# Norm rows moved into shared pages, sign-weight loads asked for one piece ahead, and the first score steps of an image ordered step by step

## The chip, the core and the metric

The kernel runs on one core of a Trainium2 chip. The metric is device time in microseconds (us) for one execution of the whole program. The profile comes from one further execution, recorded by the hardware profiler. A core has a matrix engine (TensorE, PE in the profile, with its weight loads as PEld), a vector engine (VectorE, DVE), an activation engine (ScalarE, ACT), a general engine (GpSimd, POOL) and a queue engine (SyncE, SP) that only issues transfers. Each runs its own instructions in order and waits on semaphores for the others. TensorE's results land in PSUM, which this kernel uses as eight tiles ("banks") of 128 x 512 floats.

## The reference: what is computed

Eight images of 32 x 32 pixels (1024 tokens) with 384 channels go through two layers. All is float32.

```python
# layer 0: x = x + attention0(group_norm(x))
qkv = gn(x) @ qkv_w + qkv_b                      # 6 heads of 64
attn = einsum('bqd,bkd->bqk', q * 64**-0.5, k)   # 1024 x 1024 per head
attn = attn + rel_h[:, :, :, :, None] + rel_w[:, :, :, None, :]   # position part, from q
x = x + softmax(attn) @ v @ proj_w + proj_b
# layer 1, on tokens t (8, 1024, 384):
t = t + causal_attention(ln(t), Wq, Wk, Wv)      # one head of 384
t = t + ffn(ln(t), W1, b1, W2, b2)               # first 5 images only get a non-zero ffn
# ffn: both weights are replaced by the sign of (w - mean of its group of rows),
#      5 groups by output feature; after each product an absmax scale over a whole image
Wb[g] = sign(W[g] - W[g].mean())
```

(In the feed-forward part the quantization works on groups of one image for images 0 to 4; images 5 to 7 get zeros there.)

## The kernel before

A scheduler places the instructions of each engine in an order that it works out from priorities (the order in which the program asks) and from readiness, and it hands out pool buffers as they come free. An instruction that asks for a buffer waits until the buffer's last user is done. The pools that matter here:

```python
class Pools:
    def __init__(self, ctx, tc, path):
        ...
        self.image_ = pool("image", 11)                        # [128, 3080] floats each
        self.page_ = pool("page", 12 if self.fast else 8)      # [128, 1024] floats each
        self.xn = pool("xn", 3)                                # [128, 384] floats each
        ...
        self.ps_o = pool("ps_o", 8, space=PSUM)                # the eight banks
```

The signs of the feed-forward weights are made once, during image 0, by a generator that the attention code advances with `next` between its own steps. Every weight is read twice: once for the group sums (`"w"`), once for the signs (`"sign"`). The results go to DRAM (`w1s`, `w2s`) and are read back for each image.

```python
PIECES = (                                   # 1.5 MB; 0.75 + 0.75 MB; 1.5 MB
    ((0, w1T, w1s, 0, CUT1, FF),),
    ((0, w1T, w1s, CUT1, NC, FF), (1, w2T, w2s, CUT2, NM, C)),
    ((1, w2T, w2s, 0, CUT2, C),),
)
def binarize(pools):
    def pieces(name):
        for n, piece in enumerate(PIECES):
            room, at = pools.flat(f"{name}_{n}"), 0            # one image buffer
            for i, (which, src, sign, k0, k1, n_out) in enumerate(piece):
                w = room[:, at : ...]
                nc.gpsimd.dma_start(out=w, in_=src...)         # L227
                yield which, w, sign[...], n_out, i + 1 == len(piece)
    ...
    for which, w, _, n_out, _ in pieces("w"):
        yield False
        for g in range(NG):
            nc.vector.tensor_reduce(part[...], w[:, :, ts(g, n_out // NG)], AX.XY, ALU.add)   # L235
        ...
    nc.gpsimd.partition_all_reduce(mean, part, ...)            # L243
    for which, w, dst, n_out, last in pieces("sign"):
        ...   # per group: above = w > mean (L257); w = (w < mean) reversed-subtract above (L258)
        nc.sync.dma_start(out=dst, in_=w)                      # L265
```

The layer norms of layer 1 work on half an image, four rows of tiles each. The normalized row `xn` is transposed on TensorE (three 128 x 128 blocks) and copied out.

```python
for i, j in enumerate(js):                                     # four per half
    xn = pools.xn.tile([P, C], F32, tag="xn", name=f"xn_{name}_{j}")
    nc.vector.tensor_scalar(xn, xt[:, j, :], mv[:, i, 0:1], rs[:, i : i + 1], ALU.subtract, ALU.mult)   # L361
    transpose_tiles(xT[:, half, :, ts(i, P)], [xn[:, ts(k, P)] for k in range(NC)], ...)               # L299
```

Layer 0's attention takes head pairs p = 0, 1, 2 in turn. A **step** is one chunk of 128 keys (c) against 512 queries (half) for the two heads of the pair: its scores fill two banks. Each bank gets a product of queries and keys (L569) and a position part (L573) on top; ScalarE's exponential (L579) then frees the bank. Sixteen steps per pair come in bursts of 2, 3, 3, 3, 3, 2; behind the scores of one burst stand the value products (L590) of the burst before.

```python
def scores(p, c, half):
    sc = [pools.o_tile(...) for par in range(2)]
    for par in range(2):
        nc.tensor.matmul(sc[par], k[rows[par], p, ts(c, P)], q[rows[par], p, ts(half, 512)], start=True, stop=False)   # L569
    for par in range(2):
        nc.tensor.matmul(sc[par], unit[...], r[2 * (c // 4) + c % 2][rows[par], p, ts(half, 512)], start=False, stop=True)   # L573
    pr = pools.page(f"pr0_{b}_{p}_{c}_{half}")
    for par in range(2):
        last_exp[0] = nc.scalar.activation(pr[:, ts(par, 512)], sc[par], AF.Exp).ins      # L579
    return pr
...
if b == 0:
    signs.append(binarize(pools))
for p in range(NPAIR):
    sums = [pools.page(...) for half in range(2)]
    for n, burst in enumerate(bursts):
        prs = [scores(p, *u) for u in burst]
        if b == 0 and (p, n) == (0, 1):
            multiply_out(pools)        # wqk = Wq Wk^T: 9 products in 3 banks (L287), copied out by VectorE (L288)
        for u in pending:
            values(*u)                 # running sum on VectorE (L587), product with v on TensorE (L590)
        if n == 0 and p > 0: few = set_aside(p - 1, *last)
        if b == 0 and xt is None and next(signs[0]) or b > 0 and (p, n) == (1, 1):
            xt = residual()            # loads x; GpSimd adds a bias (L552)
        if p == 0:
            with tc.issue_after(last_exp[0]): next(later, None)    # position parts of pairs 1 and 2: cast (L498), rest (L499), DMAs (L506)
        if n == 2 and p > 0: divide(p - 1, few)                   # a small product into one bank (L622), read by VectorE (L412)
        pending = ...
```

Of the kernel before, what the change touches and what calls it, by code (L numbers as in the profile page):

```python
# [1 line left out]

# [7 lines left out]
F32 = mybir.dt.float32  # L10
# [7 lines left out]
P = 128  # L18
B, H, W, C = 8, 32, 32, 384
# [21 lines left out]
class Pools:  # L41
    def __init__(self, ctx, tc, path):
        self.path, self.fast = path, path == "f"

        def pool(name, bufs, **kw):
            return ctx.enter_context(tc.tile_pool(name=f"{path}_{name}", bufs=bufs, **kw))

        self.image_ = pool("image", 11)
        self.page_ = pool("page", 12 if self.fast else 8)
        self.xn = pool("xn", 3)  # L50
        self.work = pool("work", 2)
        self.small = pool("small", 3)
        self.ps_o = pool("ps_o", 8, space=PSUM)
# [20 lines left out]
def conv_attn_hybrid(  # L74
# [19 lines left out]
    nc = tc.nc  # L94
# [72 lines left out]
    unit = const.tile([P, 2, HB, WB], F32R, name="unit")  # L167
# [49 lines left out]
# [6 lines that stand above are left out]
                room, at = pools.flat(f"{name}_{n}"), 0  # L223
                for i, (which, src, sign, k0, k1, n_out) in enumerate(piece):
                    w = room[:, at : at + (k1 - k0) * n_out].rearrange("p (k o) -> p k o", o=n_out)
                    at += (k1 - k0) * n_out
                    nc.gpsimd.dma_start(out=w, in_=src.rearrange("(k p) o -> p k o", p=P)[:, k0:k1, :])  # L227
                    yield which, w, sign[:, k0 * n_out : k1 * n_out], n_out, i + 1 == len(piece)

        part = const.tile([P, 2, 2, NG], F32, name="sums_w")  # L230
        times = [0, 0]
        for which, w, _, n_out, _ in pieces("w"):
            yield False
            for g in range(NG):
                nc.vector.tensor_reduce(  # L235
                    part[:, times[which], which, g : g + 1], w[:, :, ts(g, n_out // NG)], AX.XY, ALU.add
                )
            times[which] += 1
            if which == 1 or w.shape[1] > 1:
                yield False  # L240
        nc.vector.tensor_tensor(part[:, 0], part[:, 0], part[:, 1], ALU.add)
        mean = const.tile([P, 2, NG], F32, name="mean_w")
        nc.gpsimd.partition_all_reduce(  # L243
            mean.rearrange("p a g -> p (a g)"), part[:, 0].rearrange("p a g -> p (a g)"), P, bass_isa.ReduceOp.add
        )
        for which, n in enumerate((FF // NG * C, C // NG * FF)):
            nc.vector.tensor_scalar_mul(mean[:, which], mean[:, which], 1.0 / n)
        done = 0
        for which, w, dst, n_out, last in pieces("sign"):
            gs = n_out // NG  # L250
            step = min(C // gs, w.shape[1])
            for k in range(0, w.shape[1], step):
                for g in range(NG):
                    wg, m = w[:, k : min(k + step, w.shape[1]), ts(g, gs)], mean[:, which, g : g + 1]
                    above = pools.xn.tile([P, C], F32, tag="xn", name=f"above_{which}_{n_out}")
                    above = above[:, : wg.shape[1] * gs].rearrange("p (k o) -> p k o", o=gs)
                    nc.vector.tensor_scalar(above, wg, m, None, ALU.is_gt)  # L257
                    nc.vector.scalar_tensor_tensor(wg, wg, m, above, ALU.is_lt, ALU.subtract, reverse1=True)  # L258
                    done += wg.shape[1] * gs
                    if done > 600:  # L260
                        done = 0
                        yield False
            if NG * gs < n_out:
                nc.vector.memset(w[:, :, NG * gs :], 0.0)
            nc.sync.dma_start(out=dst.bitcast(F32), in_=w.rearrange("p k o -> p (k o)"))  # L265
            if last:
                yield True
# [22 lines left out]
    def stages(pools):  # L290
# [3 lines left out]
        def transpose_tiles(dst, srcs, engine):  # L294

            n = len(srcs)
            pt = pools.o_tile("pt")
            for i, s in enumerate(srcs):
                last_transpose[0] = nc.tensor.transpose(pt[:, ts(i, P)], s, ident).ins  # L299
            engine(dst, pt[:, : n * P].rearrange("p (i q) -> p i q", i=n))  # L300
# [37 lines left out]
        def layer_norm_T(xt, xT, half, name, xlo=None):  # L338

            js = range(4 * half, 4 * half + 4)  # L340
            mv = pools.small.tile([P, 4, 2], F32, tag="lmv", name=f"lmv_{name}_{half}")
            for i, j in enumerate(js):
                st = pools.small.tile([P, 6], F32, tag="lst", name=f"lst_{name}_{j}")
                nc.vector.bn_stats(st, xt[:, j, :])
                nc.vector.bn_aggr(mv[:, i, :], st)
            sd = pools.small.tile([P, 4], F32, tag="lsd", name=f"lsd_{name}_{half}")
            nc.vector.tensor_scalar_add(sd, mv[:, :, 1], 1e-5)
            nc.scalar.activation(sd, sd, AF.Sqrt)
            rs = pools.small.tile([P, 4], F32, tag="lrs", name=f"lrs_{name}_{half}")
            nc.vector.reciprocal(rs, sd)  # L350

            def hi_lo(i):
                def place(dst, ps):
                    nc.scalar.copy(dst, ps)
                    nc.vector.tensor_tensor(xlo[:, half, :, ts(i, P)], ps, dst.bitcast(F32), ALU.subtract)

                return place

            for i, j in enumerate(js):
                xn = pools.xn.tile([P, C], F32, tag="xn", name=f"xn_{name}_{j}")  # L360
                nc.vector.tensor_scalar(xn, xt[:, j, :], mv[:, i, 0:1], rs[:, i : i + 1], ALU.subtract, ALU.mult)  # L361
                transpose_tiles(
                    xT[:, half, :, ts(i, P)], [xn[:, ts(k, P)] for k in range(NC)], nc.scalar.copy if xlo is None else hi_lo(i)
                )
            return rs
# [62 lines left out]
        def layer0(b, xT):  # L428


            q, k = (pools.image(f"{n}_{b}") for n in ("q", "k"))


            r = [pools.image(f"r_{b}_{part}", F32R) for part in range(4)]

            rows = (slice(0, HD), slice(HD, P))
# [87 lines left out]
            for m in range(2 * NPAIR):  # L524
                queries_keys(m)
                if 0 < m <= NPAIR:
                    near.append(positions(m - 1))
                if m == NPAIR and unfinished:
                    unfinished.pop()()

                    early = pools.small.tile([P, 1], F32, tag="early", name=f"early0_{b}")
                    nc.scalar.activation(early, k[:, 0, T - 1 :], AF.Exp, scale=0.0)
            for j in range(NJ):
                values(j)
            for _ in place(0, *near[0]):
# [21 lines left out]
        def attend0_fast(residual, b, q, k, r, v, later):  # L557
# [2 lines left out]
            oT = pools.image(f"oT_{b}")  # L560

            rows = (slice(0, HD), slice(HD, P))
            last_exp = [None]

            def scores(p, c, half):

                sc = [pools.o_tile(f"s0_{b}_{p}_{c}_{half}_{par}") for par in range(2)]
                for par in range(2):
                    nc.tensor.matmul(  # L569
                        sc[par], k[rows[par], p, ts(c, P)], q[rows[par], p, ts(half, 512)], start=True, stop=False  # L570
                    )
                for par in range(2):
                    nc.tensor.matmul(  # L573
                        sc[par], unit[rows[par], c // 2 % 2].rearrange("i h w -> i (h w)"),
                        r[2 * (c // 4) + c % 2][rows[par], p, ts(half, 512)], start=False, stop=True,
                    )
                pr = pools.page(f"pr0_{b}_{p}_{c}_{half}")
                for par in range(2):
                    last_exp[0] = nc.scalar.activation(pr[:, ts(par, 512)], sc[par], AF.Exp).ins  # L579
                return pr  # L580
# [59 lines left out]
                    nc.vector.tensor_tensor(oT[:, p, ts(half, 512)], avs[half], rb[:, ts(half, 512)], ALU.mult)  # L640

            xt = None
            if b == 0:
                signs.append(binarize(pools))

            units = [(c, half) for c in range(NJ) for half in range(2)]
            bursts = [units[at : at + n] for at, n in zip(BURSTS_AT, BURSTS)]
# [1 line left out]
            for p in range(NPAIR):  # L649
# [19 lines left out]
                last = (sums, avs)  # L669
# [71 lines left out]
        def attention1(xt, more, b, between, start):  # L741
# [14 lines left out]
            for j in range(7):  # L756
                more(j)
            layer_norm_T(xt, xT, 0, f"1_{b}")
            for j in range(7, NJ):
                more(j)  # L760
# [209 lines left out]
        signs = []  # L970
        unfinished = []

        def run(pools):
# [5 lines left out]
            if pools.fast:  # L979
                make_unit(pools)  # L980
            for b in range(B):
                xt, more = layer0(b, gn)

                def between():
# [32 lines left out]
    with ExitStack() as scope:  # L1017
        pools = Pools(scope, tc, "f")
# [43 lines left out]
```

## Time and profile before

| what | value |
|---|---|
| median of three executions | 2452.15 us (2447.83 to 2455.35) |
| span of the profiled execution | 2457.7 us |
| ScalarE busy | 1032.6 us (42%) |
| VectorE busy | 1393.6 us (57%) |
| GpSimd busy | 275.2 us (11%) |
| mean granted TensorE clock | 0.990 |
| period of one image: a projection of layer 0 (L423) in image 1 to the same one in image 2 (388.63 to 715.93 us) | 327.30 us |
| image 0: score steps of layer 0 to its output projection (72.13 to 205.06 us) | 132.9 us |
| image 1: the same stretch (429.07 to 532.95 us) | 103.9 us |

Read it so: busy time is what an engine's own records cover; a busy TensorE may still be running its products in a poor order, because the ends of pipelined products are modelled. The waits list tells, for each engine, what ended its idle times. The timeline gives start, length and, in square brackets, the idle time just before. A number after x is a count of instructions; one float32 product is two of them, one of the float32r products one. L numbers are lines of the kernel.

### The profile page before, as it was taken

The page shows a single profiled execution, that of the slowest core. Times are in us where ns is not written, and L with a number is a line of the kernel's source. Part 1 is how long each engine was busy: PE and PEld are TensorE (multiplying, and loading weights), DVE is VectorE, ACT ScalarE, POOL GpSimd, SP SyncE. Part 2 cuts the span into 40 slices and gives each one's busy share as a digit, 9 for nine tenths or more (in the row PEclk, how much of TensorE's full clock was granted, in tenths as well). Part 3 has the DMA queues.
Part 4 walks back from the last instruction along what each step waited for, and adds up shares of the span by engine and source line. Part 5 has one row for each costly group of instructions (what it writes and reads, how often), then busy time and mean ns, then how long its engine had stood idle before and what let it go on. Part 6 is the DMA issues. An engine that isn't in the chain of part 4 may idle for free.

```text
span 2457.7 us, 25707 instructions
## 1 busy us (share of the span) xinstructions
PE 2400.5 (98%) x9378; PEld 1286.1 (52%) x9378; DVE 1393.6 (57%) x2182; ACT 1032.6 (42%) x1756; POOL 275.2 (11%) x389
## 2 busy tenths in 40 slices
PE   7899999999999999999999999999999999999998
PEld 3334576345674356843457634567435543554344
DVE  4577555773475754557635577346575257524751
ACT  3342264632465513745226463246551155125520
POOL 0230001300013000022000130001300021001200
PEclk9899999999999999999999999999999999999999
DMA  7622206310127011082110631012700271017100
GB/s 160 197 82 99 103 1 125 107 53 12 39 77 155 27 38 39 1 172 69 55 39 1 128 104 54 12 39 77 155 26 1 64 155 40 0 43 143 47 1 28
DMA packets 154792, 169.97 MB, mean 69 GB/s; under 512 B 113408, under 2 KB 126048, under 8 KB 153120
## 3 DMA queue, kind: packets, MB, share of 16 engines
q1 hardware_dynamic: 134416, 98.93, 17.6%
q0 software_dynamic: 17184, 69.22, 9.4%
q8 instruction: 77, 1.26, 0.2%
q10 hardware_dynamic: 3056, 0.08, 0.1%
q14 instruction: 59, 0.48, 0.1%
HBM read 75.38 MB, written 42.47 MB: 48 GB/s over the span
## 4 chain that ended last, share of the span: by engine, by line
PE 95%; DVE 2%; DMA 1%; ACT 1%; issue 0%; POOL 0%; DVEq 0%; ACTq 0%
PE f_s L569 14%; PE f_av L590 14%; PE f_qk L423 10%; PE f_av L805 8%; PE f_s L792 8%; PE f_y L952 7%; PE f_y L911 7%; PE f_v L371 5%; PE f_v L518 5%; PE f_q L749 5%; PE f_s L573 4%; PE f_pj L371 2%; PE f_rel L468 2%; PE f_pj L679 2%; PE f_pt L299 1%; PE f_pj L684 1%
## 5 line engine op out<-in xcount | busy, mean ns | idle before, releaser
L579 ACT ACTIVATE f_pr<-f_s 128x512 f32<-128x512 f32 x768 | 409.2, 597 | 351.8 <-PE f_s L573 295.6
L569 PE MATMUL f_s<-f_q,f_k 64*128 64x512 f32 x1536 | 417.8, 611 | 21.3 <-DVE wqk L288 10.6
L590 PE MATMUL f_av<-f_pr,f_v 128*64 128x512 f32 x1536 | 363.8, 607 | 0.0
L587 DVE TENSOR_TENSOR f_sum<-f_sum,f_pr 128x1024 f32<-128x1024 f32 x288 | 353.8, 1279 | 17.6 <-ACT f_pr L579 17.4
L573 PE MATMUL f_s<-f_r,unit 64*128 64x512 f32 x768 | 310.6, 773 | 0.0
L423 PE MATMUL f_qk<-f_gnT,wqkv_sb 128*128 128x512 f32 x576 | 258.3, 601 | 1.6 <-DVE f_gnT L334 1.6
L569 PEld LDWEIGHTS f_s<-f_q,f_k 64*128 64x128 f32 x1536 | 147.2, 186 | 193.5 <-issue 110.6
L590 PEld LDWEIGHTS f_av<-f_pr,f_v 128*64 128x64 f32 x1536 | 99.1, 137 | 221.5 <-issue 197.2
L805 PE MATMUL f_av<-f_v,f_pr 128*128 128x385 f32 x576 | 203.8, 503 | 0.0
L792 PE MATMUL f_s<-f_q,f_lnT 128*128 128x512 f32 (+3 forms) x576 | 195.9, 488 | 0.0
L423 PEld LDWEIGHTS f_qk<-f_gnT,wqkv_sb 128*128 128x128 f32 x576 | 108.2, 191 | 143.8 <-issue 133.5
L799 ACT ACTIVATE f_pr<-f_s 128x512 f32<-128x512 f32 (+3 forms) x96 | 47.1, 490 | 262.7 <-DVE f_s L797 216.3
L805 PEld LDWEIGHTS f_av<-f_v,f_pr 128*128 128x128 f32 x576 | 112.2, 197 | 81.7 <-issue 19.7
L506 POOL DMA_DIRECT2D f_r<-f_far x192 | 101.3, 530 | 444.7 <-DVE f_far L499 378.0
L792 PEld LDWEIGHTS f_s<-f_q,f_lnT 128*128 128x128 f32 x576 | 102.0, 190 | 77.7 <-issue 54.0
L915 ACT ACTIVATE f_h<-f_y,b_sb 128x256 f32<-128x256 f32 x240 | 100.6, 470 | 67.7 <-PE f_y L911 67.7
L749 PE MATMUL f_q<-f_lnT,wqk 128*128 128x512 f32 x288 | 127.5, 592 | 0.0
L573 PEld LDWEIGHTS f_s<-f_r,unit 64*128 64x128 f32 x768 | 80.5, 188 | 89.7 <-issue 88.7
L371 PE MATMUL f_v<-wv_sb,f_lnT 128*128 128x384 f32 x384 | 126.5, 486 | 0.0
L922 DVE TENSOR_REDUCE am<-f_h 128x1 f32<-128x1024 f32 (+2 forms) x80 | 71.6, 947 | 96.3 <-ACT f_h L915 96.3
L518 PE MATMUL f_v<-wqkv_sb,f_gnT 128*128 128x384 f32 x384 | 125.1, 486 | 0.0
L806 DVE COPY tot<-f_av 128x1 f32<-128x1 f32 x64 | 10.0, 157 | 166.5 <-PE f_av L805 166.5
(162 smaller groups left out, 3071.8 us busy)
## 6 DMA issues: line engine op xcount, KB each, us to landing
f_far<-f_far SPq DMA_DIRECT2D x48, 512.0 KB, 3.4
f_r<-f_far POOLq DMA_DIRECT2D x192, 128.0 KB, 4.1
f_r<-f_far SPq DMA_DIRECT2D x192, 128.0 KB, 3.3
f_gnT<-in_xT SPq DMA_DIRECT2D x24, 512.0 KB, 4.6
f_x<-in_x SPq DMA_DIRECT2D x32, 384.0 KB, 6.3
out_y<-f_x POOLq DMA_DIRECT2D x28, 384.0 KB, 4.6
f_near<-f_far SPq DMA_DIRECT2D x128, 64.0 KB, 4.4
f_w1a<-w1s POOLq DMA_DIRECT2D x5, 1536.0 KB, 7.0
```

The lines of the kernel that those rows point to most:

```text
L371: nc.tensor.matmul(ps[:, :C], xT[:, k, ts(j, P)], w[:, k, cols], start=(k == 0), stop=(k == NC - 1))
L423: nc.tensor.matmul(made[half], wqkv_sb[:, i, ts(m, P)], xT[:, i, ts(half, 512)], start=(i == 0), stop=(i == NC - 1))
L518: nc.tensor.matmul(ps, keys[:, i, j // 2, j % 2], wqkv_sb[:, i, 2 * C :], start=(i == 0), stop=(i == NC - 1))
L569: nc.tensor.matmul(sc[par], k[rows[par], p, ts(c, P)], q[rows[par], p, ts(half, 512)], start=True, stop=False)
L573: nc.tensor.matmul(sc[par], unit[rows[par], c // 2 % 2].rearrange("i h w -> i (h w)"), r[2 * (c // 4) + c % 2][rows[par], p, ts(half, 512) ...
L579: last_exp[0] = nc.scalar.activation(pr[:, ts(par, 512)], sc[par], AF.Exp).ins
L587: nc.vector.tensor_tensor(sums[half], prev, pr, ALU.add)
L590: nc.tensor.matmul(avs[half][ts(par, HD), :], v[:, c, ts(h, HD)], pr[:, ts(par, 512)], start=(c == 0), stop=(c == NJ - 1),)
L749: nc.tensor.matmul(ps, wqk[:, k, ts(m, P)], xT[:, half, k, :], start=(k == 0), stop=(k == NC - 1))
L792: nc.tensor.matmul(sc[:, lo:], xT[:, c // 4, k, ts(c % 4, P)], q[:, half, k, lo:], start=(k == 0), stop=(k == NC - 1),)
L805: nc.tensor.matmul(av[:, : C + 1], prs[c][:, ts(j - c, P)], v[:, c, :], start=(c == 0), stop=(c == j))
L911: nc.tensor.matmul(ps, w1k[i // 2][:, ts(m, P)], xs[i % 2][:, half, i // 2, :], start=(i == 0), stop=(i == 2 * NC - 1))
```

## The change

Four edits are made together.

- The norm rows `xn` are taken from the page pool (12 buffers) instead of from a pool of their own with 3. That pool keeps 2 buffers for the sign work.
- The loads of weights, for sums and for signs, are asked for one piece ahead of the piece being worked on (`one_ahead`).
- For image 0 the generator is started in front of layer 0's value projection, not at the start of the attention, so that its first loads are asked for there.
- In each image's first pair, steps 1 to 4 are tied behind the last position part of the step before: the scheduler may no longer put the query-key products of later steps ahead of an earlier step's position part.

```diff
-        self.xn = pool("xn", 3)
+        self.xn = pool("xn", 2)
...
+        def one_ahead(loads):
+            got = next(loads)
+            for load in loads:
+                yield got
+                got = load
+            yield got
...
-        for which, w, _, n_out, _ in pieces("w"):
-            yield False
+        loads = one_ahead(pieces("w"))
+        got = next(loads)
+        yield False
+        for which, w, _, n_out, _ in itertools.chain([got], loads):
             for g in range(NG):
...
-        for which, w, dst, n_out, last in pieces("sign"):
+        for which, w, dst, n_out, last in one_ahead(pieces("sign")):
...
             for i, j in enumerate(js):
-                xn = pools.xn.tile([P, C], F32, tag="xn", name=f"xn_{name}_{j}")
+                xn = pools.page(f"xn_{name}_{j}")[:, :C]
...
+            if pools.fast and b == 0:
+                signs.append(binarize(pools))
+                next(signs[0])
             for j in range(NJ):
                 values(j)                       # layer 0's value projection
...
-            last_exp = [None]
+            last_exp, last_score = [None], [None]
             def scores(p, c, half):
                 sc = [...]
-                for par in range(2):
-                    nc.tensor.matmul(sc[par], k..., q..., start=True, stop=False)
-                for par in range(2):
-                    nc.tensor.matmul(sc[par], unit..., r..., start=False, stop=True)
+                with tc.issue_after(last_score[0]) if p == 0 and 0 < 2 * c + half < 5 else contextlib.nullcontext():
+                    for par in range(2):
+                        nc.tensor.matmul(sc[par], k..., q..., start=True, stop=False)
+                    for par in range(2):
+                        last_score[0] = nc.tensor.matmul(sc[par], unit..., r..., start=False, stop=True).ins
...
-            if b == 0:
-                signs.append(binarize(pools))
```

More of the change, by code (lines that the diff above doesn't have):

```diff
@@ L1 @@
+import contextlib
+import itertools
 from contextlib import ExitStack
@@ L562, in attend0_fast @@
             rows = (slice(0, HD), slice(HD, P))
-            last_exp = [None]
+            last_exp, last_score = [None], [None]
             def scores(p, c, half):
                 sc = [pools.o_tile(f"s0_{b}_{p}_{c}_{half}_{par}") for par in range(2)]
-                for par in range(2):
-                    nc.tensor.matmul(
-                        sc[par], k[rows[par], p, ts(c, P)], q[rows[par], p, ts(half, 512)], start=True, stop=False
-                    )
-                for par in range(2):
[L573 to L576, printed above, removed]
+                with tc.issue_after(last_score[0]) if p == 0 and 0 < 2 * c + half < 5 else contextlib.nullcontext():
+                    for par in range(2):
+                        nc.tensor.matmul(
+                            sc[par], k[rows[par], p, ts(c, P)], q[rows[par], p, ts(half, 512)], start=True, stop=False
+                        )
+                    for par in range(2):
+                        last_score[0] = nc.tensor.matmul(
+                            sc[par], unit[rows[par], c // 2 % 2].rearrange("i h w -> i (h w)"),
+                            r[2 * (c // 4) + c % 2][rows[par], p, ts(half, 512)], start=False, stop=True,
+                        ).ins
                 pr = pools.page(f"pr0_{b}_{p}_{c}_{half}")
```

## The prediction

> **What bounds the kernel now.** I read the busy table first, then TensorE's waits, then timelines of the places that the change touches. In the busy table the columns are busy time, share of the span and instructions:
>
> ```profile
> span 2457.7 us, 25707 instructions
> PE 2400.5 (98%) x9378; PEld 1286.1 (52%) x9378; DVE 1393.6 (57%) x2182; ACT 1032.6 (42%) x1756; POOL 275.2 (11%) x389
> ```
>
> TensorE is idle for 2457.7 - 2400.5 = 57.2 us only. So no edit that merely fills idle time can bring more than 57 us (2.3%), and the waits say who holds what part of it (total us, times, longest):
>
> ```profile
> PE f_pt L299 <- DVE xn L361: 12.4, 13, 2.0
> PE f_gmean L321 <- DVE gmv L318: 11.3, 1, 11.3
> PE f_s L569 <- DVE wqk L288: 10.6, 1, 10.6
> PE f_s L569 <- ACT f_pr L579: 6.7, 15, 0.5
> PE f_s L569 <- DVE seen L412: 4.0, 1, 4.0
> ```
>
> Lines 1, 3, 4 and 5 belong to the three things changed: norm rows, weight loads (image 0), first score steps. The timeline of TensorE shows more than idle time. Where image 1's scores begin, the scheduler has put the query-key products of four steps ahead of the first position part (start, length; idle before in brackets):
>
> ```profile
> 429.07 3.70 PE L569 MATMUL f_s<-f_q,f_k 64*128 64x512 f32 x16
> 432.21 1.04 PE L573 MATMUL f_s<-f_r,unit 64*128 64x512 f32 x4
> 433.69 1.18 PE L569 MATMUL f_s<-f_q,f_k 64*128 64x512 f32 x3 [0.44 <-ACT f_pr L579]
> ...
> 435.46 1.94 PE L590 MATMUL f_av<-f_pr,f_v 128*64 128x512 f32 x8
> ...
> 437.33 0.73 PE L573 MATMUL f_s<-f_r,unit 64*128 64x512 f32 x4
> ...
> 438.51 1.18 PE L569 MATMUL f_s<-f_q,f_k 64*128 64x512 f32 x3 [0.45 <-ACT f_pr L579]
> ...
> 445.19 1.13 PE L569 MATMUL f_s<-f_q,f_k 64*128 64x512 f32 x4
> ```
>
> All eight banks are opened, none is finished before 432.2, so the first exponential starts at 433.04 and frees banks one at a time. The normal rhythm begins at 445.19.
>
> [...] after the 10.6 us wait twelve value products take 4.94 us, and 2.79 us later; granted clock 0.69 in 84 to 104 us. [...] here a pair of score products passes in about 0.4 us, and pairs break up where banks come free singly (433.69). [...] here a running sum takes 1.2 us, and 2.0 us while GpSimd's bias adds run (138 to 156 us).
>
> **Step 1, score order, images 1 to 7.** In the changed program as built, TensorE's order is step 0 whole, step 1 whole, and so on: the rhythm of all other pairs. From 429.07 to 445.19, 16.12 us, stand 8 score steps and 5 value steps. Their price in the normal rhythm, from distances between starts: three score steps 448.67 - 445.19 = 3.48; three value steps 451.40 - 448.67 = 2.73; two score steps 459.97 - 457.59 = 2.38; two value steps (image 0, 128.99 to 130.86) 1.87. So 2.38 + 3.48 + 1.87 + 3.48 + 2.73 = 13.94, and **2.18 us** are saved per image: 0.9 are the two waits[...]. Two conditions. ScalarE must keep up: its first exponential comes 1.45 us after the first product of a burst (457.59 to 459.04), a step's two take 1.06, and its casts (1.04 and 1.99) stay where they are; laid out from 429.07, step 4 then finds its banks free at 431.6 and needs them at 433.4, and step 7 finds its own at 437.0 and needs them at 438.9. No stall. And the position parts must have landed: parts r_0 and r_1 of pair 0 are issued last at 425.2 to 426.4 on SP and land in 2.4 to 3 us, by 429.5; they would now be wanted at 429.9 and 431.7. 7 x 2.18 = **15.3 us**.
>
> **Step 2, norm rows.** Per image with a feed-forward part the fourth transpose waits for its norm row, which waited for the first row's buffer, which TensorE frees only by transposing:
>
> ```profile
> 620.31 1.15 PE L299 MATMUL f_pt<-ident,xn 128*128 128x128 f32 x9
> ...
> 622.83 0.47 DVE L361 TENSOR_SCALAR xn<-f_x,lmv,lrs 128x384 f32<-128x384 f32 x1
> ...
> 623.45 0.52 PE L299 MATMUL f_pt<-ident,xn 128*128 128x128 f32 x3 [2.00 <-DVE xn L361]
> ```
>
> With four buffers to be had, VectorE's order puts the fourth row right behind the third, at about 616.7, 3.6 us before TensorE wants the first. 5 x 2.0 = 10.0; the other eight waits (2.4 us together, 0.3 each, in the first norm of layer 1) have the same cause. I take 11.4 of 12.4. Pages are not short there: the attention's are done with.
>
> **Step 3, image 0.** Here I expect little. The stretch from scores to output projection takes 132.9 us against 103.9 in image 1; 8.2 of the 29 are real extra products (L273 2.1, L287 6.1). The 10.6 us wait arises so: VectorE stands in its queue at the sums of the first piece, whose load was issued at 84.44 behind position-part DMAs on GpSimd and lands at 95.58, and the copies of wqk, which free three banks, stand behind the sums. In the changed order pieces 0 and 1 (3 MB) are loaded at the very start and summed by 60 us. But piece 2 stands behind the same DMAs (which wait for VectorE's L499, then at about 78), so it is issued at about 82.5 and lands at about 93.5 if it takes 11.1 us again; and VectorE's first sum of it stands **ahead** of the wqk copies still, the copies being mixed with five sums of 0.78. The last bank comes free at 94.3 + 3 x 0.49 + 4 x 0.78 = 98.9. TensorE is then through steps 6 and 7 at about 99.9, and was at 104.25 before: 4.3 gained, not 10.6.
>
> Then VectorE becomes the nearer limit. From 98.9 its order holds, ahead of pair 0's closing transposes: 14 running sums (16.5), two position remainders (3.2), the signs of pieces 0 and 1 (about 20 pairs, 14), then transposes and reductions (4.7): done at about 139 to 140. TensorE wants their result (L622) at 99.9 + 38.0 (the distance 104.25 to 142.29 before) = 137.9. It waits some 2 us, and the wait for a bank behind it (4.0 before) stays at about the same length, since GpSimd's bias adds now fall at about 137 to 155. Gain left: about 2 to 3. Against it stands the start: 3 MB from GpSimd's queue join at about 6 us the loads that hold up the first product (14.78). The scale of the projection weights ends at 12.84, 1.9 us early[...]. I put this at -1. Net for image 0: **+1**, anywhere from -5 to +8.
>
> **Sum.** 15.3 + 11.4 + 1 = 27.7 us; 2452.15 - 27.7 = **2424.4 us**, 1.1% faster.
>
> **Rivals.** (a) Position parts come late: TensorE, no longer fed with query-key products, stands at step 0 or 2. The old order hid up to 3 us of lateness; the margins above are 2 to 5 us. If it happens, step 1 gives nothing: 2440. (b) VectorE takes over in image 0, with signs ahead of running sums: pages fill, exponentials stop, TensorE waits 10 us more than I say: 2435. (c) The start is slowed by 5 us through shared transfers: 2429. (d) Piece 2 arrives early or its sums are not in the way, and the 10.6 us with its throttled clock vanishes: about 10 us more, 2414. (e) TensorE's 2.0 us waits turn into waits for ScalarE's copy out of the bank; that copy takes 0.48 us a row and is not late today, so I give this little.
>
> **Range and chances.** Steps 1 and 2 are sums of repeated, nearly equal pieces (26.7 us); I trust them to within 4. Image 0 gives the width: 2412 to 2438 for 8 in 10. Faster by over 2% means below 2403.1, a gain of 49 us, more than idle time and the reorder together can plausibly give: 0.03. Slower by over 2% would need a stall of 75 us against the gains: 0.01. Within 2%: 0.96.
>
> **What would show it.** In the profile after: no wait of L299 on xn beyond 1 us in total; no L569 wait on f_pr in images 1 to 7, and a distance from an image's first score product to its third burst's first of 14 us, not 16.12; a period from image 1 to image 2 of 327.3 - 2.2 - 2.0 - 0.3 = 322.8 us; the wait on wqk still there, at 6 to 11 us; a wait at L622 or behind it of 4 to 7 us; the first L423 product at 15 to 17 us. Wrong would be: an L573 wait on a DMA of f_r, a wqk wait of under 3 us, VectorE busy without a gap and TensorE waiting for it for more than 8 us in image 0, or a first product after 18 us.

## The result and the profile after

The changed kernel took **2424.7 us** (median of four executions, 2424.4 to 2427.3), the kernel before 2453.75 us beside it (2447.8 to 2459.3): ratio 0.9884, 95% interval 0.9859 to 0.9909. 1.2% faster, within the prediction's range and 0.3 us from its middle. The sum was right, two of its terms were too small, and the third had the wrong sign.

The busy table of the changed kernel (busy time, share of the span, instructions):

```profile
span 2422.6 us, 25725 instructions
PE 2378.5 (98%) x9378; PEld 1274.1 (53%) x9378; DVE 1392.1 (57%) x2182; ACT 1035.4 (43%) x1756; POOL 264.9 (11%) x389
```

The span is 35.1 us shorter (the profiled execution of the kernel before was one of its longer ones). Only 13.1 us of that is idle time of TensorE (57.2 to 44.1); 22.0 us is "busy" time that went although the 9378 products are the same. So most of the gain is in how fast the products pass, and that the table of busy times can't say. TensorE's waits after (total us, times, longest):

```profile
PE f_gmean L333 <- DVE gmv L330: 11.3, 1, 11.3
PE f_qk L435 <- DVE f_gnT L346: 8.4, 1, 8.4
PE f_s L585 <- DVE wqk L300: 8.3, 1, 8.3
PE f_pt L311 <- DVE f_xn L373: 2.4, 8, 0.3
PE f_s L585 <- DVE seen L424: 2.1, 1, 2.1
```

Gone are the five 2.0 us waits for norm rows and every wait of scores for exponentials. The second line has grown from 1.6 us: the first projection product of image 0 starts at 21.57 us, and not at 14.78. Third and fifth line are image 0's waits, 10.6 and 4.0 us before.

TensorE's timeline in image 1 shows the score order: a step's query-key products (L585), then its position part (L589), without a wait:

```profile
426.40 1.13 PE L585 MATMUL f_s<-f_q,f_k 64*128 64x512 f32 x4
426.96 0.80 PE L589 MATMUL f_s<-f_r,unit 64*128 64x512 f32 x2
427.60 1.02 PE L585 MATMUL f_s<-f_q,f_k 64*128 64x512 f32 x4
...
440.12 1.13 PE L585 MATMUL f_s<-f_q,f_k 64*128 64x512 f32 x4
```

From the first product to the third burst it is 440.12 - 426.40 = 13.72 us (16.12 before).

The norm rows of the feed-forward part of image 1, in the same view; first line the kernel before, behind its wait, then the kernel after:

```profile
623.80 11.58 PE L805 MATMUL f_av<-f_v,f_pr 128*128 128x385 f32 x30
```

```profile
615.09 1.47 PE L311 MATMUL f_pt<-ident,f_xn 128*128 128x128 f32 x12
616.39 9.89 PE L819 MATMUL f_av<-f_v,f_pr 128*128 128x385 f32 x30
```

The twelve transposes are one block, as foreseen. What was not foreseen: the thirty value products behind them, which nothing in the change touches, take 9.89 us and not 11.58. From the first transpose to the next projection it is 11.03 us (615.09 to 626.12), before 14.91 (620.31 to 635.22): 3.88 us per image, where the prediction had 2.0.

### The profile page after: what moved, and what is told of

Read it like the earlier page. It is cut to its first block, busy times and chain, and to the rows that moved or that the text cites. A ratio compares the mean times of both kernels' runs of the same rounds, so it can differ in the third digit from the quotient of the medians.

```text
span 2422.6 us, 25725 instructions
## 1 busy us (share of the span) xinstructions
PE 2378.5 (98%) x9378; PEld 1274.1 (53%) x9378; DVE 1392.1 (57%) x2182; ACT 1035.4 (43%) x1756; POOL 264.9 (11%) x389
## 4 chain that ended last, share of the span: by engine, by line
PE 96%; DVE 2%; DMA 1%; issue 0%; ACT 0%; POOL 0%; DVEq 0%; ACTq 0%
PE f_s L585 14%; PE f_av L606 14%; PE f_qk L435 10%; PE f_s L806 8%; PE f_av L819 8%; PE f_y L966 7%; PE f_y L925 7%; PE f_v L383 5%; PE f_v L530 5%; PE f_q L763 5%; PE f_s L589 4%; PE f_pj L383 3%; PE f_rel L480 2%; PE f_pj L693 2%; PE f_pt L311 1%; PE f_pj L698 1%
## 5 line engine op out<-in xcount | busy, mean ns | idle before, releaser
L585 PE MATMUL f_s<-f_q,f_k 64*128 64x512 f32 x1536 | 413.2, 609 | 10.4 <-DVE wqk L300 8.3
L603 DVE TENSOR_TENSOR f_sum<-f_sum,f_pr 128x1024 f32<-128x1024 f32 x288 | 360.8, 1300 | 18.6 <-ACT f_pr L595 18.2
L589 PE MATMUL f_s<-f_r,unit 64*128 64x512 f32 x768 | 309.9, 794 | 0.0
L585 PEld LDWEIGHTS f_s<-f_q,f_k 64*128 64x128 f32 x1536 | 137.9, 186 | 179.0 <-issue 105.4
L819 PE MATMUL f_av<-f_v,f_pr 128*128 128x385 f32 x576 | 195.3, 486 | 0.0
L589 PEld LDWEIGHTS f_s<-f_r,unit 64*128 64x128 f32 x768 | 75.2, 187 | 91.1 <-issue 89.8
L530 PEld LDWEIGHTS f_v<-wqkv_sb,f_gnT 128*128 128x128 f32 x384 | 75.3, 196 | 50.3 <-issue 3.5
```

Source lines behind the costliest of these rows:

```text
L530: nc.tensor.matmul(ps, keys[:, i, j // 2, j % 2], wqkv_sb[:, i, 2 * C :], start=(i == 0), stop=(i == NC - 1))
L589: last_score[0] = nc.tensor.matmul(sc[par], unit[rows[par], c // 2 % 2].rearrange("i h w -> i (h w)"), r[2 * (c // 4) + c % 2][rows[par], ...
L603: nc.vector.tensor_tensor(sums[half], prev, pr, ALU.add)
L819: nc.tensor.matmul(av[:, : C + 1], prs[c][:, ts(j - c, P)], v[:, c, :], start=(c == 0), stop=(c == j))
```

## Experiments

Each kernel ran beside the kernel before on the same chip. "Before" is its median there.

| run | what it is | us | before | ratio, 95% interval |
|---|---|---|---|---|
| e1 | before + score order | 2434.8 | 2455.0 | 0.9920 (0.9907 to 0.9934) |
| e2 | before + norm rows in pages | 2438.6 | 2455.0 | 0.9942 (0.9925 to 0.9958) |
| e3 | before + loads | 2453.0 | 2455.0 | 0.9995 (0.9985 to 1.0005) |
| e4 | before + filled wait, first try | 2453.9 | 2455.0 | 0.9995 (0.9985 to 1.0005) |
| e9 | before + filled wait, second try | 2446.2 | 2453.9 | 0.9967 (0.9956 to 0.9978) |
| e5 | after, again | 2422.9 | 2456.4 | 0.9868 (0.9850 to 0.9887) |
| e6 | after without the loads | 2418.4 | 2456.4 | 0.9850 (0.9832 to 0.9868) |
| e7 | after, first loads held back | 2418.8 | 2456.4 | 0.9847 (0.9831 to 0.9863) |
| e8 | e7 + wqk copies on ScalarE | 2413.9 | 2456.4 | 0.9833 (0.9817 to 0.9849) |
| e10 | e8 + later signs | 2415.0 | 2453.9 | 0.9840 (0.9822 to 0.9857) |
| e11 | e6 + wqk copies on ScalarE | 2417.8 | 2453.9 | 0.9854 (0.9833 to 0.9875) |
| e12 | e10 + later bias adds | 2409.4 | 2457.0 | 0.9807 (0.9793 to 0.9821) |

Theory A, formed after the result: the three parts are separate; the norm rows bring more than their wait, for a wait also lowers TensorE's clock; and the loads cost at the start what they give in image 0's attention. Rivals stand with each run.

### The parts alone (e1, e2, e3)

The edits are those of the diff above, one part at a time.

> The kernel before with the score order alone. Theory A (the parts of the change are separate and add up; the order saves 2.4 us in each of images 1 to 7, as the distance from first score product to third burst, 16.12 before and 13.72 after, says): 7 x 2.40 = 16.8 us less than before, about 2437 us, in a range of 14 to 19 us less. The norm-row waits of 2.0 us and the 10.6 us wait on wqk stay. Rival (the shorter stretch needs the other parts too, since signs, sums and pages compete with it on VectorE): under 12 us less.

Measured: 20.2 us less (16 to 23 by the interval), a little over the range that I expected. In image 1 the distance from first score product to third burst is 436.04 - 422.32 = 13.72 us, exactly that of the changed kernel; images 1 to 7 have 13.71 to 13.73 (before 16.11 to 16.13). So the order is worth 2.40 us in each of seven images, 16.8 us, by itself. Image 0 has the same order, and its waits on wqk and seen are shorter too (9.25 and 2.35 us; 11.1 and 4.2 in e2 and e4).

> The kernel before with the norm rows in pages alone. Theory A (besides the wait of 2.0 us, the wait had a price behind it: thirty value products that took 11.41 us behind it and 9.72 us without it): 5 x (2.0 + 1.7) = 18.5 us less than before, about 2435 us, and the eight waits of 0.3 us stay. The prediction's own sum: 11.4 us less, about 2442 us. Over 15 us less is for A, under 13 for the prediction's sum. In the profile A wants the thirty value products at 9.7 us and a period from image 1 to image 2 shorter by 3.7 us.

Measured: 16.5 us less. Over 15: the wait had a price behind it. All five groups of thirty value products take 9.88 or 9.89 us.

> The kernel before with the loads alone (weights asked for a piece ahead, the first 3 MB from the start on). Theory A: the first product starts at 21 to 22 us instead of 14.8 (6.8 us lost) and the attention of image 0 is 4.5 us shorter, so 2 us more than before, about 2456 us, from 0 to 5 us more; images 1 to 7 unchanged. Rival (the late first product belongs to something else, and the loads are a gain): 3 to 5 us less than before, first product before 17 us.

Measured: 2.0 us less in the medians, with equality inside the interval. Neither expectation held. The late start did: the first product starts at 21.04 us. But the attention gave back more than I thought: first scores to output projection 78.82 to 203.07, 124.3 us, against 129.8 to 130.2 in the three runs whose image 0 has neither score order nor loads (e2, e4, e9). Its wait on wqk is longer (12.64 us); what vanished is the wait on `seen`, VectorE's reductions that read the denominators' bank and so free it (4.2 us in e2 and e4), and with it a spell of lowered clock (0.97 mean from 140 to 206 us there, 1.00 here).

So by themselves the parts bring 20.2, 16.5 and 2.0 us, together 38.7; the changed kernel brings 29.05 or, beside e5, 33.5. Something is counted twice or lost. e6 says which.

### All but the loads (e5, e6)

e5 is the changed kernel again; e6 is the changed kernel with the weight loads as before (no `one_ahead`, generator started in the attention).

> The changed kernel itself once more, beside the next three. 2424 to 2427 us, first product at 21 to 22 us, wait on wqk of 8 to 9 us.

> The changed kernel with the loads put back (score order and norm rows in pages only). Theory A (the early loads cost 6.8 us at the start, and what they give back in image 0's attention is small once the score order is in, since the order alone already had the output projection of image 0 at 199.9 us against 206.4 in the changed kernel): 5 to 8 us less than the changed kernel, about 2418 us. Rival (the loads alone took 2.0 us off the kernel before, so they are a gain): 2 us more than the changed kernel or above.

Measured: 2422.9 and 2418.4 us, so 4.5 us between them, somewhat under the 5 to 8 of theory A and against the rival. Order and pages together bring 38.0 us, as much as they bring one by one (36.7). **The loads, added to these two, cost 4.5 us.** Alone they take away image 0's wait on seen; with the score order that wait is down to 2.1 us without them (e6), and with them it is 2.0 (e5). Scores to output projection: 127.6 us in e6, 128.5 in e5. So nothing is gained in the attention to pay for the late start.

### The clock behind a 2 us wait (e4, e9)

Why do thirty untouched products pass faster? e4 leaves the wait and fills it:

```diff
 def transpose_tiles(dst, srcs, engine, fill=0):
     ...
     engine(dst, pt[:, : n * P]...)
+    for _ in range(fill):                  # 15, behind the third row of each feed-forward norm
+        nc.tensor.transpose(pt[:, ts(3, P)], ident, ident)
```

> The kernel before, with fifteen more transposes of the identity behind the third norm row's in each feed-forward image, into columns of the bank that nothing reads: they fill about 1.8 us of the 2.0 us in which TensorE waits for the fourth norm row, and the wait itself stays. Output unchanged. Theory A (the thirty value products behind the wait are slow since the idle time lowers the granted clock, 0.69 in 624.0 to 629.5 us): they take 9.7 instead of 11.4 us, 5 x 1.7 = 8.5 us less than before, about 2445 us, though TensorE does more work. Rival (they are slow for another reason that the wait comes with: the 1.6 MB of transfers in that stretch, or late operands): same time as before, products at 11.4 us, clock 0.69 again.

Measured: the same time as before, as the rival had it, but the products fast in all five images, as theory A had it. TensorE's timeline in image 1 of e4 says why both are true:

```profile
616.05 1.15 PE L299 MATMUL f_pt<-ident,xn 128*128 128x128 f32 x9
618.70 1.85 PE L302 MATMUL f_pt<-ident 128*128 128x128 f32 x15 [1.51 <-DVE f_lnlo L357]
620.39 0.49 PE L299 MATMUL f_pt<-ident,xn 128*128 128x128 f32 x3
620.72 9.89 PE L808 MATMUL f_av<-f_v,f_pr 128*128 128x385 f32 x30
```

The fill waited itself for VectorE to read the bank and so stood mostly behind the gap: it shortened the idle time to 1.5 us only, and put the fourth row 1.2 us later. That eats what the clock gave. e9 puts the fifteen transposes into the fourth row's bank, free early:

```diff
     pt = pools.o_tile("pt")
+    for _ in range(fill):                  # 15, ahead of the fourth row
+        nc.tensor.transpose(pt[:, ts(3, P)], ident, ident)
     for i, s in enumerate(srcs): ...
```

> The kernel before once more with fifteen idle transposes in each feed-forward image, this time into the bank of the fourth norm row's transposes, which is free early, so that they (and one value product that the order places with them) stand in the 2.0 us wait and not behind it. Output unchanged. Theory A (a 2.0 us idle time sometimes lowers the clock for the next 5.5 us at a cost of 1.7 us): no wait over 0.5 us there, all five groups of value products at full clock, 5 us less than the kernel before at the average of some four throttled gaps of five (up to 8.5), about 2449 us, and the fourth norm row where it was: the 10 us of waiting are still spent. Rival (the first filled run was fast for another reason): slow products again, or the same time as the kernel before.

Measured: 7.7 us less than before, with 75 products more. No wait for norm rows is left in the feed-forward part (the eight of 0.3 us stay). Image 1 of e9:

```profile
615.54 1.15 PE L301 MATMUL f_pt<-ident,xn 128*128 128x128 f32 x9
616.53 1.80 PE L299 MATMUL f_pt<-ident 128*128 128x128 f32 x15
618.16 0.81 PE L808 MATMUL f_av<-f_v,f_pr 128*128 128x385 f32 x2
618.81 0.49 PE L301 MATMUL f_pt<-ident,xn 128*128 128x128 f32 x3
619.14 9.24 PE L808 MATMUL f_av<-f_v,f_pr 128*128 128x385 f32 x28
```

From the first transpose to the next projection 12.68 us pass (615.54 to 628.22); before it was 14.91. The order also moved two value products into the gap, worth 14.91 - 1.69 - 12.68 = 0.54 us; the rest, 1.69 us, is clock.

The clock itself stands in the view by windows, third column from the end (ahead of it each window's length and the busy times of five engines, behind it the transfers). The kernel before, behind its wait in image 1:

```profile
623.50:624.00 0.50, 0.50 (x4) 0.49 (x5) 0.45 (x2) 0.00 (x0) 0.00 (x0) 1.00 1.03 406
624.00:624.50 0.50, 0.50 (x2) 0.27 (x1) 0.00 (x0) 0.48 (x1) 0.00 (x0) 0.51 0.99 381
...
626.50:627.00 0.50, 0.50 (x2) 0.20 (x1) 0.00 (x0) 0.00 (x0) 0.00 (x0) 0.50 0.00 0
627.00:627.50 0.50, 0.50 (x3) 0.20 (x2) 0.00 (x0) 0.00 (x0) 0.00 (x0) 0.58 0.00 0
627.50:628.00 0.50, 0.50 (x3) 0.32 (x2) 0.00 (x0) 0.00 (x0) 0.00 (x0) 1.00 0.00 0
```

It falls to 0.50 at 624.0 and is back at about 627.4 us. One stretch of 3.4 us at half speed costs 1.7 us, which is 11.58 - 9.89. And it does not come every time. TensorE's timeline of e1, images 1 and 2, the same instructions behind the same wait:

```profile
614.27 0.52 PE L301 MATMUL f_pt<-ident,xn 128*128 128x128 f32 x3 [1.99 <-DVE xn L363]
614.62 11.58 PE L808 MATMUL f_av<-f_v,f_pr 128*128 128x385 f32 x30
...
939.12 0.52 PE L301 MATMUL f_pt<-ident,xn 128*128 128x128 f32 x3 [1.99 <-DVE xn L363]
939.48 9.89 PE L808 MATMUL f_av<-f_v,f_pr 128*128 128x385 f32 x30
```

Of fifteen such gaps in three traces nine were followed by slow products (five of five in the trace of the kernel before, two of five in e1, two of five in e3); of the five gaps of 1.5 us in e4 and the five filled ones in e9, none. Nine of fifteen is 0.6; from e9's time, (7.7 / 5 - 0.54) / 1.69 = 0.59 (0.3 to 1.0 by its interval).

In the kernel before, the five spells behind the norm rows start at 296.33, 624.01, 951.69, 1279.37 and 1607.05 us, each 327.68 us after the last, and each is 3.41 us long at 0.50. Here is the one of image 1, in the view by windows:

```profile
624.01:627.42 3.41, 3.41 (x6) 1.68 (x5) 0.56 (x1) 0.47 (x1) 0.00 (x0) 0.50 0.25 96
```

What decides whether the products behind a wait are slow was not shown: no run here moved such a wait and changed nothing else. One image takes 327.30 us in the kernel before, so that its five cases are nearly one case repeated, and I estimate that its five of five says little more than one draw; e1 and e3 had 4 of 10.

The spells may explain a part of the spread of the kernel before (27 executions from 2450.1 to 2461.8 us; e4, which differs in the gaps alone, had fourteen from 2452.4 to 2456.2), but not all of it: e2, which has none of these gaps, had six from 2436.3 to 2444.2.

### The late start (e7)

```diff
+                    if name == "w" and n == 0:
+                        nc.gpsimd.tensor_copy(w[:, 0, 0:1], wqkv_sb[:, 0, 0:1])   # scaled weights
                     nc.gpsimd.dma_start(out=w, in_=...)
```

> The changed kernel, with one GpSimd copy of one column of the scaled projection weights into the first weight tile ahead of its load, so that the 3 MB start when the projection weights have landed and are scaled (about 13 us) instead of at 5.3 us. Theory A (the first product is late since the 3 MB share the DMA engines with the projection weights): first product back at 14.5 to 15.5 us, and 5 to 7 us less than the changed kernel, about 2418 us. Rival (something else at the start is late, or the later 3 MB push back the position parts): no change, or first scores later.

Measured: 4.1 us less than e5, a little under what I expected, and the first product at 15.41 us. The DMA issues of the first 30 us (size of one, median us from issue to landing), first of the changed kernel, then of e7:

```profile
wqkv_sb<-in_qkv_w SPq DMA_DIRECT2D x3, 576.0 KB, 13.8
f_w<-in_w1T POOLq DMA_DIRECT2D x1, 1536.0 KB, 9.3
```

```profile
wqkv_sb<-in_qkv_w SPq DMA_DIRECT2D x3, 576.0 KB, 7.0
f_w<-in_w1T POOLq DMA_DIRECT2D x1, 1536.0 KB, 10.4
```

Without the 3 MB beside them the projection weights take 7.0 us, with them 13.8, while the large transfer lands in 9.3 us all the same. ScalarE's timeline of the changed kernel shows who is made to wait, idle time in brackets:

```profile
19.13 1.16 ACT L136 ACTIVATE wqkv_sb<-wqkv_sb 128x1152 f32<-128x1152 f32 x1 [9.90 <-DMA wqkv_sb<-in_qkv_w]
```

The scale of the weights starts at 12.97 us in e7. In the first 40 us of e5 GpSimd's queue moved 3.15 MB in 608 packets, 5.2 KB each, and SP's 5.91 MB in 2978, 2.0 KB each. Why the one transfer is late and the other not was not shown: no run here varied the packets' size.

### Image 0's wait on wqk (e8, e10, e11, e12)

The wait of 8.3 us is VectorE's queue: the copies of wqk stand among the sums of the third piece of weights, which lands at 100.7 us. e8 moves the copies.

```diff
-            nc.vector.tensor_scalar_mul(wqk[:, m, :], ps[:, :C], C**-0.5)
+            nc.scalar.mul(wqk[:, m, :], ps[:, :C], C**-0.5)
```

> The kernel of the run before it, with the three copies of wqk out of their banks put on ScalarE instead of VectorE, so that they no longer stand behind the sums of the third piece of weights. Theory A (TensorE's wait on wqk is VectorE's queue, and the slow products behind it are its clock): the 8.3 us wait falls under 1 us, but the running sums still stand behind the third piece's sums until about 104 us, and the 12 pages fill: a part of it comes back as waits for exponentials. 3 to 8 us less than the run before it. Rival (VectorE is the bound of image 0 anyway): under 2 us less, with waits on VectorE of the same length later on.

Measured: 4.8 us less than e7. The wait is gone and comes back further on, as TensorE's timeline shows (waits in brackets):

```profile
102.82 2.07 PE L587 MATMUL f_s<-f_q,f_k 64*128 64x512 f32 x3 [2.97 <-ACT f_pr L597]
139.53 0.43 PE L640 MATMUL f_den<-few,fold 128*64 128x32 f32 x4 [7.42 <-DVE f_sign L278]
```

On waits the rival was right: those on wqk, exponentials, denominators and `seen` are 10.8 us together in e8, against 11.0 in e7. What shrank is TensorE's work at half clock in image 0, from 15.0 us to 9.9, which is 2.6 of the 4.8 us. The denominators of pair 0 wait for VectorE, which has some twenty sign operations ahead of the transposes that close the pair. e10 asks for the signs three bursts later:

```diff
         done = 0
+        for _ in range(3):
+            yield False
         for which, w, dst, n_out, last in one_ahead(pieces("sign")):
```

> The kernel with held loads and wqk copies on ScalarE, with the signs asked for three bursts later, so that VectorE's order has them behind the transposes and reductions that close pair 0, and not ahead of them. Theory A (the 7.4 us wait ahead of the denominators in that run is the price of some twenty sign operations ahead of them): that wait falls under 2.5 us, output projection of image 0 at 192 to 194 us instead of 197.3, and 3 to 5 us less than that run, about 2410 us. Rival (VectorE's sums and remainders alone hold pair 0 back, or the later signs make the same wait at the next pair's end): under 2 us less.

Measured: no gain (ratio 0.9840 against 0.9833, intervals overlapping), the rival's outcome. The wait became one of 12.06 us, on `seen` behind the denominators' reciprocal, again VectorE:

```profile
141.43 1.19 PE L589 MATMUL f_s<-f_q,f_k 64*128 64x512 f32 x1 [12.06 <-DVE seen L428]
```

e11 takes the other way, e6 with the ScalarE copies:

> Score order and norm rows in pages, the loads as in the kernel before, and the copies of wqk on ScalarE: the loads part is left out altogether. VectorE's order has the signs behind the close of pair 0 here, but the sums of pieces 0 and 1 ahead of the first running sum. Theory A: the wait of 8.6 us on wqk goes, about 3 to 5 us come back as waits for exponentials or denominators: 2412 to 2416 us, a little slower than the run above since ten sums more stand on VectorE in the attention. Rival (early sums matter more than that): 2416 or above, no better than without the ScalarE copies.

Measured: ratio 0.9854, no better than e6 (0.9850): waits of 0.97 and 3.07 us for exponentials and 10.57 us on seen. So in image 0 of these runs TensorE follows VectorE, whichever operation was moved. In e10 VectorE's timeline held a hint, however: its operations themselves were slow just there. First e10, while GpSimd's bias adds run (127.78 to 139.9 us), then the same operations in e12:

```profile
131.70 2.45 DVE L274 SCALAR_TENSOR_TENSOR f_sign<-f_sign,mean_w,above 128x307 f32<-128x307 f32 x2
134.07 1.10 DVE L273 TENSOR_SCALAR above<-f_sign,mean_w 128x307 f32<-128x307 f32 x1
135.09 3.94 DVE L607 TENSOR_TENSOR f_sum<-f_pr,f_pr 128x1024 f32<-128x1024 f32 x2
```

```profile
130.62 0.98 DVE L274 SCALAR_TENSOR_TENSOR f_sign<-f_sign,mean_w,above 128x307 f32<-128x307 f32 x2
131.52 0.37 DVE L273 TENSOR_SCALAR above<-f_sign,mean_w 128x307 f32<-128x307 f32 x1
131.81 2.35 DVE L611 TENSOR_TENSOR f_sum<-f_pr,f_pr 128x1024 f32<-128x1024 f32 x2
```

e12 holds the bias adds behind the division that closes pair 0, and asks for x and the adds in the fourth burst of pair 1:

```diff
+                held = pools.small.tile([P, 1], F32, ...)
+                last = nc.gpsimd.tensor_copy(held, oT[:, 0, 0:1]).ins
+                with tc.issue_after(last):
                     for j in range(NJ):
                         nc.gpsimd.tensor_tensor(xt[:, j, :], xt[:, j, :], pb, ALU.add)
```

> The kernel of the late-signs run, with GpSimd's eight bias adds of image 0 (127.78 to 139.9 us there) held behind the division that closes pair 0, by a GpSimd copy of one column of its result. Nothing is left out. Theory A (VectorE is the bound there, and while the adds run its operations take nearly twice as long: running sums 2.0 us instead of 1.2, sign comparisons 1.1 instead of 0.37): from 129.6 to 140.9 us some 5 us are saved, so the 12.06 us wait ahead of pair 1's scores falls to 6 to 8 us, and 3 to 6 us less than that run, about 2410 us, unless the adds slow pair 1 in turn. Rival (the wait is set by the load of x or by another transfer, or the adds cost the same wherever they stand): under 2 us less.

Measured: ratio 0.9807 against 0.9840, intervals apart (5.6 us in the medians, 8 by the ratios); the output projection of image 0 starts at 190.51 us (197.04 in e10, 206.43 in the changed kernel), and the wait is half as long:

```profile
135.75 1.19 PE L593 MATMUL f_s<-f_q,f_k 64*128 64x512 f32 x1 [6.01 <-DVE seen L428]
```

From the two comparisons ahead of the first line of each fence to the reciprocal VectorE runs the same operations in both, in 11.26 us in e10 (129.63 to 140.89) and in 5.16 in e12 (130.05 to 135.21), and that difference is the wait's. The load of x is not the cause: it is issued from 117.1 us in e10 and from 117.5 in e12. e12 leaves nothing out of the computation and is the fastest of all: 2409.4 us, 1.9% less than the kernel before. The adds run from 149.4 us there, and slow VectorE as much (a running sum at 152.84 takes 2.02 us), but TensorE does not wait for it at that place.

## Why the prediction was right, and where it was wrong

- **Score order: right, a little small.** 2.18 us per image foreseen, 2.40 measured (16.12 to 13.72). The term that was mis-sized is the first five score steps: priced as two bursts at 2.38 + 3.48 = 5.86 us, they pass as one in 5.66 (426.40 to 432.06). There was no stall of ScalarE and there were no late position parts (no such line among the waits). Left out: the same order in image 0, where it shortened the two waits as well. e1 gives 20.2 us for the whole part, against 15.3.
- **Norm rows: the mechanism right, the term too small.** The 2.0 us waits went, as foreseen. The step that failed is "I take 11.4 of 12.4": the wait was counted at its length. The slow products behind it came in nine of fifteen cases, 1.7 us each, so that the part is worth 15 to 17 us (e2: 16.5; worked out, 5 x (3.88 - 0.4 x 1.69) = 16.0). I had read that effect in the trace for the 10.6 us wait and did not look at the products behind the 2.0 us waits, where 11.58 us for thirty stood on record. For the same reason the ceiling of 57 us on what filling idle time can bring was none: a filled gap can also make the products behind it faster (9.89 us in e4 for 11.58). The smaller mistake in the same step: the eight waits of 0.3 us do not have the same cause; all eight are still there, 2.4 us, where the text wanted under 1 us in total. Each image has one, at a third norm row, for which VectorE is late since it puts a residual add of 0.55 us (L701) between the second row and the third (at 220.47 us in image 0).
- **Image 0: the sign wrong.** Foreseen: -1 at the start and +2 to +3 in the attention, net +1. Measured, with the other parts in: -4.5 (e5 against e6). The start's term, the step that failed, was mis-sized: 6.8 us late (21.57 against 14.78), outside the 15 to 17 us that the text named for the first product, and past the 18 us that it said would be wrong. That was rival (c), 5 us, which I had not given enough weight. In the attention one wait was to be shortened and one to stay. The first came out, the wait on wqk with 8.3 us (6 to 11 foreseen); the second did not, since the one behind the denominators is 2.1 (4 to 7 foreseen). But the part of it that the loads earn is about nil, since the score order alone shortens the same waits (8.6 and 2.1 us in e6). The third piece, expected to land at about 93.5 us, was there at 100.7.
- **The sum** was 27.7 us and the result 29.05: too little for the norm rows and the order, by some 11 us (38.0 measured in e6 against 26.7), too much for image 0 by 5.5. They offset each other in part only: 27.7 + 11.3 - 5.5 = 33.5, the gain of e5. The 29.05 is less since the kernel before was 2.6 us faster in the median there and the changed one 1.8 us slower. That the first result fell on the middle of the range is luck, and no proof of the steps.
- Period from image 1 to image 2: 321.2 us (616.39 to 937.63), foreseen 322.8; the difference is about the 1.7 us of clock.

What stays open is the clock behind image 0's long waits. In every trace the stretch from first score to output projection is TensorE's idle time, plus half of the time that it works at half clock, plus 109.1 to 110.7 us: 15.0 + 7.8 of the first two in the kernel before, 10.6 + 7.5 in the changed one, 13.1 + 2.0 in e3, 10.8 + 6.1 in e6, 6.7 + 2.8 in e12. So the early loads leave the idle time where the score order alone puts it, and of the 5.6 us that they gave in e3 some 1.9 are clock (e2 and e4 have 3.9). Behind the wait on wqk the clock stayed at 0.50 for 11 us after TensorE had resumed in the changed kernel (102 to 113 us) and for 4 us in e3 (108 to 112), and no run here controlled it.

## What to carry to other kernels

A wait of TensorE costs its length and perhaps slow products behind it (here 1.7 us behind nine of fifteen waits of 2.0 us): compare the products behind a wait with equal ones elsewhere before you put a price on it. A load that is moved to an earlier time can collide with what is loaded then (here 13.8 us instead of 7.0 for the projection weights); look first at what the first product waits for, and hold the new load behind that. Where several waits belong to one engine's queue, moving one operation moves the wait; look for what makes that engine's operations slow at that place (here GpSimd's adds: 11.26 us for what took 5.16 without them).

## What the runs showed of the hardware that I had not expected

- An idle time of TensorE of 2.0 us was followed by slow products in nine of fifteen cases (11.57 or 11.58 us for thirty that take 9.89 otherwise), in the five of the kernel before with the clock at 0.50 for 3.41 us; one of 1.5 us was in none of five.
- 3 MB in GpSimd's queue beside three loads of 0.6 MB in SP's (the changed kernel against e7): the three took 13.8 us in the median instead of 7.0, the first 1.5 MB of the 3 MB 9.3 instead of 10.4.
- VectorE under GpSimd's bias adds (e10 against e12): a comparison with one tensor input went from 0.37 to 1.1 us, one with two from 0.53 to 1.2, a running sum from 1.2 to 2.0. The prediction had the running sum; that the shorter operations suffer by a factor of two to three was new, and keeping clear of it was worth 6 to 8 us in e12.
